# Queries and keys of three of four head groups as seven block products, in a transformer block of attention and feed-forward

## The chip, the cores and the metric

The kernel runs on one core of a Trainium2 chip. Five engines work side by side, each through its own list of instructions in order: TensorE (PE in the profile; PEld is its loading of weights), VectorE (DVE), ScalarE (ACT), GpSimd (POOL) and SyncE (SP), whose queue issues nearly all transfers. TensorE writes its results into PSUM, eight banks of 128 partitions x 512 floats; DVE and ACT read them there. The metric is the device time of one execution in microseconds, the median of several runs.

## The reference, cut to what matters

All numbers are 32-bit floats. B = 8 sequences of S = 1024 rows, D = 512 columns, H = 16 heads of 32.

```python
x = L0_attn_h                                     # (8, 1024, 512)
# attention, on the layer-normed x
qvk = (h @ Wqvk).reshape(b, s, 3, H, HD)
q, v, k = (qvk[:, :, 0], qvk[:, :, 1], qvk[:, :, 2])
scores = einsum('bshi,bthi->bsth', q, k) + causal_mask
weights = softmax(scores / sqrt(d), axis=2)
wv = einsum('bsth,bthi->bshi', weights, v).reshape(b, s, d)
x = x + layernorm(wv @ Wo)
# feed-forward, on the layer-normed x: W1, a sine transform with per-column parameters, relu, W2
x = x + layernorm(ffn(layernorm(x)))
```

The change is about `q` and `k`: for a group of four heads they are two products of the normed x (1024 x 512) with 128 columns of the weights each.

## The kernel before, in words

One sequence after the other; in each, attention over four groups of four heads (`attention`, L770), then the output projection and norm (`finish_block`, L871), then the feed-forward layer (`feed_forward`, L942). The normed x of a sequence lies transposed in SBUF, as `xnT[b, half]`: 128 partitions x 4 blocks of the contraction (`kc`) x 512 rows, for each half of the sequence. It is made during group 2 of the sequence before (`norm1`).

The order of the work is written by hand. Each engine does its instructions in the order in which the program issues them (`in_order`), and PE's stream is woven from generators: `advance(work, n)` issues the next n steps of one. `work` is the projection of the next group's queries, values and keys (`project_qkv`, L461); its steps are put between the steps of the present group's attention, so that PE has something to do while other engines read PSUM.

A group goes through these stages:

1. *The maxima* (`find_maxima`, L536). The softmax needs the maximum of each row beforehand. `run_unit` (L564) takes a *unit*: for the four heads of a group, 128 queries against up to 512 keys, four matmuls on 32 rows of the array each (L575), into two pairs of PSUM banks. A piece (i, c) is query block i against half c of the keys. DVE then reads the banks: a reduction where no mask is needed (L593), a masked one otherwise (L605). For the first half of the queries ACT also sums exponentials (L625). The units stand in four runs (`MAX_RUNS`, L520), and after run n come `MAX_FILL` steps of `work` (L529). The maxima are then split into three bfloat16 parts (`split`, L548; on POOL for the first half of the queries, on DVE for the second) and transposed on PE (`transpose_maxima`, L658, recorded at L115).
2. *The weights* (`weigh`, L667). A unit here is one or two key blocks against up to 512 queries: PE subtracts the transposed maxima (L681) and adds the scores (L692), ACT takes the exponential (L707), POOL zeroes what lies above the diagonal (L711). One unit later PE multiplies the weights with the values (`weighted_values`, L730), and DVE adds them up for the row sums (`add_weights`, L759). There are three units for the first half of the queries and seven for the second (`KEY_UNITS`).
3. Two units of the second half's maxima (`MAX_LATE`, L526: (7,1) and (7,0)) are done late, ahead of the first two units of weights. The first also has steps of `work` behind it. After the second one DVE splits the maxima (L556 to L562), and PE transposes the parts after the third unit of weights.
4. *The sums* (`whole`, L745): PE sums the weights over the partitions. This is issued after the first run of the next group's maxima, and ACT and DVE divide by it.

PSUM is given out by the program (`psum`, L85): it takes the free bank, or pair of banks, that was given back (`drained`, L104) longest ago in program order. A matmul into a bank waits until the last reader of what lay there has finished. In `project_qkv` the bank of a half of the queries or keys is taken, filled by four matmuls and emptied by ACT in one go (L477, L488).

The feed-forward layer already computes its two products by blocks, seven products for eight, with sums of the weights made once and stored (`w1_mixed`, `w2_mixed`), sums of the moving operand on POOL (`mix`, L925; `blocks`, L1121) and sums of the results on DVE (`add`, L1078 and L1155).

Weights come through a pool of 18 tiles (`wp`), fetched group by group (`fetch`, L142) and, for the feed-forward layer, as a stream up to 16 deep. Most large tiles come from the pool `pp` (19).

Of the kernel before, what the change touches and what calls it, by code (L numbers as in the profile page):

```python
# [32 lines left out]
def kernel(  # L33
# [34 lines left out]
    pp = ctx.enter_context(tc.tile_pool(name="pp", bufs=19))  # L68
# [3 lines left out]
    mixp = ctx.enter_context(tc.tile_pool(name="mixp", bufs=2))  # L72
# [61 lines left out]
    w2_mixed = dram.tile([NSTEP, len(PRODUCTS2), P, 2 * QUART], F32, tag="w2m", name="w2_mixed")  # L134
    wqvk_v = w_qvk.rearrange("(kc p) n -> p kc n", p=P)
# [6 lines left out]
    def fetch(b, g, queue=nc.sync):  # L142

        for part in (0, 1, 2):
            w_of[b, g, part] = w_tile([KC, P], "wqvk")
            c0 = part * D + g * P
            queue.dma_start(w_of[b, g, part], wqvk_v[:, :, c0 : c0 + P])

# [250 lines left out]

    moments_ahead = {}  # L400
# [60 lines left out]
    def project_qkv(b, g):  # L461
# [11 lines left out]
        def queries_or_keys(n, half):  # L473
            pq = psum([P, HALF])
            for kc in range(KC):
# [9 lines left out]
                if kc == 1:  # L485
                    yield True
# [3 lines left out]
            yield True  # L490

        def values(t0):
# [13 lines left out]
            drained(pv)  # L506
            yield True

        yield from queries_or_keys(0, 0)
        yield from values(0)  # L510
        yield from queries_or_keys(1, 0)
        yield from queries_or_keys(0, 1)
        yield from queries_or_keys(1, 1)
        for t0 in (2, 4, 6):
            yield from values(t0)

# [5 lines left out]
        (((6, 0),), ((4, 1), (6, 1))),  # L524
    )
    MAX_LATE = (((7, 1),), ((7, 0),))  # L526


    MAX_FILL = ((3, 2, 2, 2), (1, 2, 2, 2))  # L529
# [240 lines left out]
    def attention(b, wvT, after):  # L770
# [24 lines left out]
        for g in range(NG):  # L795
            more, first = after(g)
            mT, later = find_maxima(b, g, work, sums, more if first is None else iter(()))
            mTs = [mT]
            at = 0
            for c in range(2):  # L800
# [3 lines left out]
                for u, keys in enumerate(units):  # L804
                    later(at)
                    weights, placed = weigh(b, g, c, keys, mTs[c])
                    if at < 2:
                        advance(work)
                    if at == 2:
# [8 lines left out]
                    if c and u >= len(units) - 2:  # L818
# [52 lines left out]
    def finish_block(b, half, wvT, x2T, mixed, out_w):  # L871
# [3 lines left out]
        mixed[half] = mixp.tile([P, 3, 2, QUART], F32, tag="mix", name=f"mix_{b}_{half}")  # L875
# [49 lines left out]
        def mix(t):  # L925
# [6 lines left out]
            m1, m2, m4 = (mixed[half][:, n, :, t * P : (t + 1) * P] for n in range(3))  # L932
# [9 lines left out]
    def feed_forward(b, x2T, mixed, before, between):  # L942
# [49 lines left out]
        def product(bank, s, name, first=False):  # L992
# [7 lines left out]
                "4": m[:, 2],  # L1000
                "5": m[:, 0],
                "6": m[:, 1],
# [249 lines left out]
        finish(before)  # L1252
        units = second()
        advance(units)
        for s, quota in enumerate(SECOND):
# [3 lines left out]
            for n, more in enumerate(quota):  # L1259
# [9 lines left out]
                if s == STEPS and n == 3 and b + 1 < B:  # L1269
                    fetch(b + 1, 1)  # L1270
        finish(measuring)
        while len(quarters) > 1:
            advance_ends(1)
# [5 lines left out]
    for _ in range(TPB):  # L1279
        advance(work)  # L1280
# [75 lines left out]
```

## Time and profile before

| | |
|---|---|
| median of 3 runs | 3681.8 us (3679.7 to 3681.83) |
| the profiled execution | 3681.3 us, its span 3679.6 us |
| mean granted TensorE clock | 0.997 |
| matmuls of queries and keys (L477) | 481.3 us busy, 512 matmuls of 512 columns (recorded as 1024) |
| score matmuls for the maxima (L575) | 322.0 us |
| DVE's reading of them (L593, L605) | 309.8 and 432.5 us |
| one attention group of sequence 2 | 53.84 us, of which PE 53.61, DVE 39.93, ACT 32.55, POOL 10.14 busy |

A 32-bit matmul is recorded as two instructions, so the counts of PE are twice those of the program. Busy time of PE is the time in which any matmul is under way; the four matmuls of a unit, on 32 rows each, run side by side. A row of a timeline gives start, length, engine, line, operation, what it writes and reads, and how many instructions were merged; in brackets stand the idle time before it and the engine that ended it.

### The profile page before, as it was taken

Reading aid. Unit: us, or ns where it says so; the run is one execution under the profiler, and the core shown is the slowest. Engines: PE = TensorE matmul, PEld = TensorE weight load, DVE = VectorE, ACT = ScalarE, POOL = GpSimd, SP = SyncE. Lnnn points to the kernel's source line nnn. Section 1 sums busy time; section 2 is a strip of 40 time slices with the busy share of each in tenths; the row PEclk is TensorE's granted clock in tenths of the full one; section 3 lists DMA queues with packets and bytes.
Section 4 is the critical chain, followed back from the end, with each engine's and each line's share of the span. In section 5 each row is a group of like instructions: output and inputs, shape, how many; then the busy total and the mean of one; then the engine's idle time right before and its main releaser. Section 6 shows DMA issues by size and latency. Waiting matters only on the chain.

```text
span 3679.6 us, 61558 instructions
## 1 busy us (share of the span) xinstructions
PE 3601.1 (98%) x22721; PEld 2357.4 (64%) x22721; DVE 2680.4 (73%) x5571; ACT 1408.2 (38%) x2708; POOL 1133.8 (31%) x1740
## 2 busy tenths in 40 slices
PE   8999999999999999999999999999999999999998
PEld 4447864478654786548854488544885458854587
DVE  5877867678676786767867678776787767777775
ACT  4552135621355213652146521465114642156410
POOL 2333432134311343113431234222342223422243
PEclk9999999999999999999999999999999999999999
DMA  4444751047510574105841068310683116820176
GB/s 137 142 141 132 243 192 34 20 146 249 175 41 10 158 258 154 41 10 172 266 132 41 13 185 269 112 41 18 198 275 92 38 33 199 262 70 13 47 220 197
DMA packets 305084, 476.21 MB, mean 129 GB/s; under 512 B 29136, under 2 KB 90640, under 8 KB 304784
## 3 DMA queue, kind: packets, MB, share of 16 engines
q1 hardware_dynamic: 302624, 470.44, 40.8%
q8 instruction: 181, 2.97, 0.3%
q10 hardware_dynamic: 2160, 1.84, 0.2%
q14 instruction: 119, 0.97, 0.1%
HBM read 440.70 MB, written 31.46 MB: 128 GB/s over the span
## 4 chain that ended last, share of the span: by engine, by line
PE 83%; DVE 11%; ACT 2%; POOL 2%; issue 1%; DMA 0%; POOLq 0%; DVEq 0%; SPq 0%; ACTq 0%
PE banks L1144 16%; PE banks L1009 15%; PE banks L477 13%; PE banks L575 8%; PE banks L730 7%; PE banks L692 7%; PE banks L497 7%; PE banks L897 6%; PE banks L681 3%; PE banks L115 2%; DVE u L1036 2%; DVE hid L1052 2%; DVE u L1030 1%; PE banks L745 1%; DVE hid L1058 1%; ACT w L707 1%
## 5 line engine op out<-in xcount | busy, mean ns | idle before, releaser
L707 ACT ACTIVATE w<-banks 128x1024 f32<-128x1024 f32 (+1 forms) x640 | 566.6, 939 | 296.1 <-PE banks L692 296.0
L759 DVE TENSOR_TENSOR w<-w 128x1024 f32<-128x1024 f32 (+3 forms) x400 | 421.9, 1099 | 186.7 <-PE banks L730 151.8
L711 POOL TENSOR_SCALAR_AFFINE_SELECT w<-w 128x256 f32<-128x256 f32 x512 | 287.3, 578 | 847.2 <-ACT w L707 839.8
L605 DVE CUSTOM_DVE_ANT_0 es<-banks,mask 128x128 f32<-128x128 f32 (+3 forms) x1024 | 432.5, 485 | 102.6 <-PE banks L575 102.6
L1009 PE MATMUL banks<-x2T,wm 128*128 128x256 f32 x2048 | 477.3, 381 | 28.1 <-DVE u L1079 13.6
L477 PE MATMUL banks<-xnT,wqvk 128*128 128x512 f32 x1024 | 481.3, 609 | 0.7 <-ACT xnT L342 0.7
L1144 PE MATMUL banks<-wm,hm 128*128 128x256 f32 x2048 | 470.4, 380 | 2.3 <-POOL hm L1125 2.3
L1037 ACT ACTIVATE u<-u 128x1024 f32<-128x1024 f32 x128 | 135.3, 1057 | 852.1 <-DVE u L1036 803.5
L1009 PEld LDWEIGHTS banks<-x2T,wm 128*128 128x128 f32 x2048 | 386.7, 190 | 91.0 <-DVE u L1079 16.8
L1144 PEld LDWEIGHTS banks<-wm,hm 128*128 128x128 f32 x2048 | 388.0, 190 | 56.4 <-POOL hm L1125 5.5
L593 DVE TENSOR_REDUCE mx<-banks 128x1 f32<-128x512 f32 (+1 forms) x384 | 309.8, 862 | 109.1 <-PE banks L575 109.1
L1144 PE MATMUL banks<-wm,hid 128*128 128x256 f32 x1536 | 357.7, 379 | 0.0
L1009 PE MATMUL banks<-mix,wm 128*128 128x256 f32 x1536 | 354.6, 380 | 2.3 <-DVE u L1079 2.3
L1125 POOL TENSOR_TENSOR hm<-hid 128x256 f32<-128x256 f32 x256 | 204.0, 797 | 456.2 <-DVE hid L1058 437.9
L477 PEld LDWEIGHTS banks<-xnT,wqvk 128*128 128x128 f32 x1024 | 182.8, 190 | 239.1 <-issue 184.5
L692 PE MATMUL banks<-q,k 32*128 32x512 f32 (+3 forms) x3072 | 329.6, 491 | 0.0
L730 PE MATMUL banks<-w,v 128*32 128x512 f32 (+3 forms) x3072 | 318.5, 495 | 5.4 <-POOL w L711 5.4
L1009 PEld LDWEIGHTS banks<-mix,wm 128*128 128x128 f32 x1536 | 291.1, 190 | 50.6 <-issue 7.6
L575 PE MATMUL banks<-k,q 32*128 32x512 f32 (+3 forms) x3072 | 322.0, 513 | 0.4 <-DVE mx L605 0.2
L1144 PEld LDWEIGHTS banks<-wm,hid 128*128 128x128 f32 x1536 | 292.4, 190 | 39.1
L625 ACT ACTIVATE es<-es,mx 128x512 f32<-128x512 f32 (+3 forms) x512 | 279.6, 550 | 2.1 <-DVE mx L605 2.1
L497 PEld LDWEIGHTS banks<-wqvk,xnT 128*128 128x128 f32 x2048 | 239.3, 192 | 51.6 <-issue 24.4
(114 smaller groups left out, 4322.9 us busy)
## 6 DMA issues: line engine op xcount, KB each, us to landing
wm<-w_mixed SPq DMA_DIRECT2D x1344, 256.0 KB, 3.1
xin<-in_L_attn_h_dram SPq DMA_DIRECT2D x112, 256.0 KB, 3.8
wqvk<-in_L_attn_Wqvk_dram SPq DMA_DIRECT2D x93, 256.0 KB, 5.2
out_dram<-x SPq DMA_DIRECT2D x64, 256.0 KB, 2.1
x<-in_L_attn_h_dram SPq DMA_DIRECT2D x60, 256.0 KB, 3.1
w_mixed<-w_t SPq DMA_DIRECT2D x56, 256.0 KB, 3.0
wo<-in_L_attn_Wo_dram SPq DMA_DIRECT2D x32, 256.0 KB, 5.0
w_t<-in_L_ffn_W_dram SPq DMA_DIRECT2D x32, 128.0 KB, 4.0
```

Source lines behind the costliest of these rows:

```text
L477: nc.tensor.matmul(pq, w_of[b, g, 2 * n][:, kc, :], xnT[b, half][:, kc, :], start=(kc == 0), stop=(kc == KC - 1),)
L497: nc.tensor.matmul(pv[:, t - t0, :], xnT[b, t // TPB][:, kc, (t % TPB) * P : (t % TPB + 1) * P], w_of[b, g, 1][:, kc, :], start=(kc == 0), ...
L575: nc.tensor.matmul(scs[j // 2][:, j % 2, at : at + n], queries[r, i * P : (i + 1) * P], keys[r, k0 : k0 + n], start=True, stop=True,)
L593: nc.vector.tensor_reduce(out=mx[:, m], in_=sc[:, m, cols], op=ALU.min, axis=mybir.AxisListType.X,)
L605: nc.vector.tensor_tensor_reduce(out=es[:, m, cols], in0=sc[:, m, cols], in1=mask[:, HALF - n :], scale=1.0, scalar=FMAX, op0=ALU.add, op1 ...
L692: nc.tensor.matmul(sts[j // 2][:, j % 2, cols], all_keys[r, kb * P : (kb + 1) * P], all_queries[r, q0 : q0 + n], start=False, stop=True,)
L707: in_order(nc.scalar.activation(w[:, :, :width], st[:, :, :width], AF.Exp, scale=-1.0))
L711: select = nc.gpsimd.affine_select(out=square, in_=square, compare_op=ALU.is_ge, fill=0.0, base=0, pattern=[[0, 2], [1, P]], channel_multi ...
L730: nc.tensor.matmul(acc[r, HALF - n :], v[b, g][:, kb, r], weights[j // 2][:, j % 2, cols], start=first and k == 0, stop=last and k == len( ...
L759: in_order(nc.vector.tensor_add(t[:, :, q], t[:, :, q], w[:, :, cols]))
L1009: nc.tensor.matmul(bank[:, n, :], w[:, n, kc, :], moving[:, kc, :], start=first and kc == 0 and n == 0, stop=kc == 1 and n == 1, skip_grou ...
L1144: nc.tensor.matmul(region, a[:, n], w[:, n], start=start and n == 0, stop=last and n == 1, skip_group_check=True,)
```

## The change

For groups 1 to 3 of every sequence, queries and keys are computed together. With the two halves of the sequence, the two halves of the contraction, and queries and keys as the two halves of the result, they are a product of two 2 x 2 block matrices, and the change computes it as seven block products (two matmuls of 512 columns each) with sums of blocks before and after, instead of eight:

- the sums of the x blocks (`mix_x`): four tiles, made once for a sequence by eight POOL subtractions, at the end of the feed-forward layer of the sequence before; they stay for three groups;
- the sums of the weight blocks (`mix_weights_of_group`): made once, in the first sequence, by four POOL operations for each group, and stored in DRAM; later sequences load them as two more tiles with a group's weights;
- the sums of the results (`quarters`): PE accumulates in place in three banks, `one`, `two` and `three`, over four steps; `one` is held over two steps, `two` over four, `three` over three. DVE makes five additions from PSUM, ACT three copies for four before. Group 0 is computed as before.

The steps of `work` are regrouped: there is no step of half a projection any more, one step holds two block products (or one and two blocks of values), and `MAX_FILL` gives one step to each run (two to the first, in group 0). Values for rows 0 to 255 become the first step, which is issued with the last unit of weights of the group before; the step that stood with the second-last unit is gone, and so is the step between the first and second late unit.

One unit of the maxima, (6,0), leaves the fourth run and becomes a third late unit, issued behind the second unit of weights and the last values; the split of the second half's maxima follows it.

The feed-forward layer's sums of x move from a pool of their own to `pp`, which grows from 19 to 24 tiles.

```diff
@@ project_qkv
+        def quarters():
+            ...
+            one = psum([P, HALF])
+            product(one, wq, 0, xnT[b, 0][:, :2, :], True)
+            in_order(nc.scalar.copy(p1, one))
+            two = psum([P, HALF])
+            product(two, s12, 2, t2, True)
+            add(u2, two, p1)
+            in_order(nc.scalar.activation(u2s, u2, AF.Copy, scale=-QSCALE))
+            yield True
+            product(one, wq, 2, xnT[b, 0][:, 2:, :])
+            in_order(nc.scalar.activation(queries[:, near], one, AF.Copy, scale=-QSCALE))
+            drained(one)
+            three = psum([P, HALF])
+            product(three, s12, 0, t1, True)
+            yield True
+            product(two, s34, 0, t3)
+            add(u3, two, p1)
+            add(keys[:, far], three, u3)
+            values(2)
+            yield True
+            product(two, wk, 2, t4)
+            add(keys[:, near], two, p1)
+            drained(two)
+            product(three, s34, 2, xnT[b, 1][:, 2:, :])
+            in_order(
+                nc.vector.scalar_tensor_tensor(
+                    queries[:, far], three, -QSCALE, u2s, ALU.mult, ALU.add
+                )
+            )
+            drained(three)
+            yield True
+
+        values(0)
+        yield True
+        if g == 0:
+            ...
+        else:
+            yield from quarters()
+        for t0 in (4, 6):
+            values(t0)
+            yield True
@@
-        (((6, 0),), ((4, 1), (6, 1))),
+        (((4, 1), (6, 1)),),
     )
-    MAX_LATE = (((7, 1),), ((7, 0),))
-    MAX_FILL = ((3, 2, 2, 2), (1, 2, 2, 2))
+    MAX_LATE = (((7, 1),), ((7, 0),), ((6, 0),))
+    MAX_FILL = ((2, 1, 1, 1), (1, 1, 1, 1))
@@ attention
-                    later(at)
+                    if at < 2:
+                        later(at)
                     weights, placed = weigh(b, g, c, keys, mTs[c])
-                    if at < 2:
+                    if at == 1:
                         advance(work)
+                        later(at + 1)
...
-                    if c and u >= len(units) - 2:
+                    if c and u == len(units) - 1:
                         advance(work)
```

## The prediction

> **What bounds the kernel now.** I read the page first (engine shares, then the chain that ended last), then cut one attention group of sequence 2 (53.84 us, 1014.98 to 1068.82) into windows, then read the order in time of TensorE (PE) and VectorE (DVE) in it, and last the idle times of PE with the granted clock.
>
> ```profile
> PE 3601.1 (98%) x22721; PEld 2357.4 (64%) x22721; DVE 2680.4 (73%) x5571; ACT 1408.2 (38%) x2708; POOL 1133.8 (31%) x1740
> ...
> PE 83%; DVE 11%; ACT 2%; POOL 2%; issue 1%; DMA 0%; POOLq 0%; DVEq 0%; SPq 0%; ACTq 0%
> ```
>
> PE is busy 98% of the span: work taken from PE is worth its full duration only while no new wait takes its place. The windows of the group (columns: length, then busy time and count of PE, weight loads, DVE, ACT, POOL, then the granted PE clock):
>
> ```profile
> 1014.98:1020.97 5.99, 5.99 (x58) 3.28 (x57) 4.76 (x20) 3.05 (x10) 0.00 (x0) 1.00 0.00 0
> 1020.97:1026.54 5.57, 5.57 (x37) 2.73 (x33) 4.87 (x12) 4.27 (x14) 0.00 (x0) 1.00 0.00 0
> 1026.54:1032.11 5.57, 5.57 (x37) 2.51 (x33) 5.17 (x20) 3.46 (x12) 0.00 (x0) 1.00 0.13 34
> 1032.11:1037.80 5.69, 5.69 (x33) 3.57 (x29) 4.39 (x18) 2.01 (x7) 1.44 (x6) 1.00 0.21 60
> 1037.80:1049.10 11.30, 11.30 (x125) 6.91 (x124) 6.95 (x18) 6.06 (x9) 2.82 (x8) 1.00 0.15 42
> 1049.10:1068.80 19.70, 19.47 (x180) 6.71 (x176) 13.77 (x14) 13.70 (x16) 5.88 (x9) 1.00 0.13 45
> ```
>
> The first four windows are the maxima stage. PE never waits there, but DVE is busy 4.4 to 5.2 of some 5.6 us: the two run in step, and PE is covered only because it has projections to do (L477, L497) while DVE reads the scores. The order in time shows how tight this is:
>
> ```profile
> 1019.04 2.00 PE L575 MATMUL banks<-k,q 32*128 32x512 f32 x16
> 1020.97 3.70 PE L477 MATMUL banks<-xnT,wqvk 128*128 128x512 f32 x8
> 1024.60 2.00 PE L575 MATMUL banks<-k,q 32*128 32x512 f32 x24
> ...
> 1041.93 1.14 PE L575 MATMUL banks<-k,q 32*128 32x512 f32 x8
> ...
> 1047.77 0.40 PE L115 MATMUL banks<-ident_h,parts_q 128*128 128x128 bf16 x4
> ```
>
> ```profile
> 1020.20 2.42 DVE L593 TENSOR_REDUCE mx<-banks 128x1 f32<-128x512 f32 x3 [0.60 <-PE banks L575]
> ...
> 1043.08 2.42 DVE L593 TENSOR_REDUCE mx<-banks 128x1 f32<-128x512 f32 x3 [1.59 <-PE banks L575]
> ...
> 1045.54 0.23 DVE L556 TENSOR_TENSOR mx<-mx 128x16 f32<-128x16 f32 x1
> ...
> 1047.08 0.20 DVE L560 CAST parts_q<-mx 128x16 bf16<-128x16 f32 x1
> ```
>
> A unit of four heads takes PE 0.96 us (1041.93 to 1042.89); DVE begins 1.16 us after the unit's start and reduces it in 2.42 us (0.6, 0.6, 1.2 for the pair); the split into three parts ends at 1047.28. So the last late unit has its parts ready 5.35 us after it starts, and PE's transposition of them (L115) comes 5.84 us after: 0.5 us to spare.
>
> Last, two rows of what a wait costs besides itself. At 97.98 PE had stood idle 1.96 us (for a selection on POOL); 1.6 us later the granted clock is half for 3.4 us:
>
> ```profile
> 96.00:98.00 2.00, 0.04 (x4) 0.02 (x2) 1.60 (x3) 0.00 (x0) 2.00 (x3) 1.00 0.44 153
> 98.00:99.50 1.50, 1.50 (x20) 0.81 (x24) 1.50 (x2) 0.00 (x0) 1.50 (x2) 1.00 0.77 235
> 99.50:103.00 3.50, 3.50 (x19) 0.97 (x12) 3.50 (x16) 0.47 (x1) 0.45 (x1) 0.51 0.73 203
> ```
>
> The gaps of 1.69 and 1.70 us at the start of the feed-forward stage (eight of them, one for each sequence) are followed by no such fall.
>
> **What is removed.** A projection of 512 columns takes PE 3.63 us for four (1020.97 to 1024.60), 0.907 us each. Sixteen become fourteen in 24 groups (three in each of eight sequences): 48 x 0.907 = 43.6 us off PE. ACT loses one copy of four (0.60 us) for each, off the path.
>
> **What is added and moved, by the new program's order.** I count from the start of a middle group (t = 0), with the durations above.
>
> (1) Second unit pair of the maxima. The projections now keep two of the eight banks across the runs of score units (the block sums are built in place), before they kept none. In the new order unit (5,0) takes banks 2, 3 and 6, 7, and (3,0) takes 0, 1 and then 2, 3 again; before, (3,0) had four others. PE: run 0 1.08, sums 1.0, two products 3.63, so (5,0) starts at 5.7 and (3,0) could run from 6.7 to 7.65. DVE reads bank 2 until 7.5 and bank 3 until 8.1; the last head starts at 8.2 and ends at 9.05. Wait 1.4 us; the next projection, which needs the whole array, queues behind it.
>
> (2) Third run. (4,0) and (1,0)+(5,1) now use the same banks 0 to 3; before, disjoint ones. (4,0) starts 12.7, DVE reads it from 13.85 to 16.27; the second unit, which PE would do from 13.65 to 14.6, ends at 17.3. Wait 2.7 us.
>
> (3) The first transposition of the maxima: ACT's exponentials of that run now stand behind the copy of values (done 21.7), then 2.0 us of exponentials, 0.2 of Ln, 1.8 on POOL: 25.9 against PE's 25.75. Wait 0.2 us.
>
> (4) Late units (7,1) and (7,0) use the same four banks, and the values (2.0 us) that stood between them are moved behind the second. DVE needs 1.16 + 4 x 0.61 for the first; PE comes after 0.96 + 1.18: it waits 1.45 us, in all 32 groups (about 1.2 where the next sequence's transposes lie between).
>
> (5) The third late unit (6,0) with its split is now followed by one set of weighted values (1.0) and one weighing (0.65) only, and then the transposition. Ready 5.35 us after its start plus 0.1; PE is there after 0.96 + 1.0 + 0.65 = 2.6. Wait 2.85 us in the 24 groups g = 0, 1, 3; 1.85 at g = 2, where 1.04 us of transposes lies between. Queued behind: all of the second half's weighing.
>
> (6) At a group's end 3.63 us of projections became 1.98 of values. DVE's sums of weights end 7.0 us after the weighing of (5,7); PE asks for them after 1.0 + 0.65 + 1.98 + 1.43 + 1.08 = 6.15: 0.95 us, at the next two groups (g = 1, 2); between g = 2 and 3 the transposes cover it.
>
> The five new DVE operations of a group (0.69 us each, row L1079) fall into DVE's gaps: counted at nothing; without that cover 3.4 us a group. The unit taken out of the fourth run gives its 0.96 us back later, so it is neutral but for (5).
>
> By group: g = 0 1.4 + 2.7 + 0.2 + 1.45 + 2.85 = 8.6; g = 1 9.55; g = 2 1.4 + 2.7 + 0.2 + 1.2 + 1.85 + 0.95 = 8.3; g = 3 4.3. A sequence 30.75, eight of them 246 us.
>
> (7) Differences of x: eight POOL subtractions of 128x512, 1.27 us each (row L1225), at a sequence's end, where POOL has 20.4 of 37 us busy (1380 to 1417). Hidden by that idle time; bound from above, if each held up a block of the hidden layer: 10 us a sequence, 81 in all. I take 0. At the start they run beside 15 us of first projections: 0 to 5 us, I take 0. Two more weight loads of 256 KB for each group stand on SP behind all feed-forward weights, some 15 us ahead of use: 0. The block sums of the weights are made once (three times four POOL operations of 0.8 us, their stores on SP): behind them stands POOL's selection for the first values, some 6 us ahead of use: 0, at most 7. The tiles moved to the large pool leave 17 to 21 of its 24 to the work that had 19; the 17 fall in its last two steps, when most hidden tiles are used up: 0.
>
> (8) The clock. The waits of 2.7 and 2.85 us (six a sequence, 48) lie beyond the 1.96 us that halved it; a halving costs 1.7 us (half of 3.4). The clock record changes only on a raster of 3.41 us (half from 99.56 for one step and from 3400.25, 967 steps later, for three), so a wait must put about 1.96 us into one raster step: (3.41 - 1.96) + (2.8 - 1.96) = 2.3 of 3.41 positions, 67%; in (2) single heads work in between, so I take 60%: 48 x 0.6 x 1.7 = 49 us. Ends: 0, and 82 if all do.
>
> Against this row stands a rule. The Trainium skill, "TensorE: Matmul & The Clock Gate", Part 1 ("What's actually happening"), says that the clock falls to half after at least one idle window of about 3.4 us. By it none of my waits would cost more than itself and the sum would be 3884; by the row at 97.98 it is 3933.
>
> Sum against the profiled execution's own 3681.3 us (0.5 below the median of 3681.8): 3681.3 - 43.6 + 246 + 49 = **3933 us**, 6.8% slower.
>
> **Rivals.** A is the sum above: 47%.
> B, the waits come but the clock stays: 3681.3 - 43.6 + 246 = 3884. For it: the eight gaps of 1.7 us without a fall. 27%.
> C, the bank waits (1, 2, 4) are taken up, as a bank is set free by each reduction and PE has single heads to go on with; what stays is (5), 8 x (3 x 2.85 + 1.85) = 83: 3681.3 - 43.6 + 83 = 3721. Against it: PE keeps its order, and the whole-array projections stand behind. 10%.
> D, the other side: DVE has 14 us idle in a group and hides all reads, (5) too: 3681.3 - 43.6 = 3638. It decides where new waits fall below 1.82 us a group. Against it: the 5.35 us from unit to parts cannot shrink while the unit stands 2.6 us ahead. 4%.
> E, the clock falls after the 1.4 us waits as well, half of 14 a sequence: 112 x 0.5 x 1.7 = 95, or the subtractions of (7) are not hidden: 3980 to 4060. 12%.
>
> **Range and chances.** B and A with their sizes uncertain by a fifth of 246 (49 us) reach from 3835 to 3982; going towards E and somewhat towards C gives 3810 to 4020, which leaves out about 2 in 10. A measurement of this kernel can tell about 0.2% (7 us). Faster 0.04 (D), same 0.01, slower 0.95.
>
> **What would show it.** PE idle time rises from 79 us to over 250 and its busy time falls to some 3560; waits of the score matmuls and of the parts' transposition on DVE come up in PE's list of waits, some 24 x 4 and 32 x 2.8 us; the granted clock's mean falls below 0.99 (A) or stays at 0.997 (B). Wrong would be: the group after still at 52 us without idle PE (D), or the third run without a wait (C).

## The result: 3944.2 us, 7.1% slower

The changed kernel takes 3944.2 us (median of 4 runs, 3940.5 to 3947.5) against 3681.8 us before: 1.0713 times as long, 95% interval 1.0695 to 1.0732. The forecast was 3933. The profiled execution of the changed kernel has a span of 3938.8 us and a mean granted clock of 0.986 (before 3679.6 and 0.997).

From the page of the kernel after, engine shares, the chain that ended last, and two of its groups (busy time and mean ns of one, then the idle time before them):

```profile
PE 3742.9 (95%) x22625; PEld 2397.1 (61%) x22625; DVE 2772.5 (70%) x5691; ACT 1394.8 (35%) x2684; POOL 1224.7 (31%) x1816
...
PE 78%; DVE 14%; POOL 3%; ACT 3%; issue 2%; DMA 0%; SPq 0%; POOLq 0%; DVEq 0%; ACTq 0%
...
L672 PE MATMUL banks<-k,q 32*128 32x512 f32 (+3 forms) x3072 | 453.6, 533 | 29.2 <-DVE mx L690 29.1
...
L690 DVE TENSOR_REDUCE mx<-banks 128x1 f32<-128x512 f32 (+1 forms) x384 | 311.7, 862 | 172.9 <-PE banks L672 172.5
```

PE has 96 instructions fewer, and its busy time *rose* by 142 us, although some 44 us of products are gone. Most of the increase, 131.6 us, is in the score matmuls of the maxima (L672, L575 before, 322.0 us), whose number is the same; the scores and weighted values of the weights stage add 26 and 24.5 us. A unit is four heads on 32 rows of the array each; when two heads run and the other two wait for their banks, PE counts as busy. Only 29 us of these waits appear as idle time. So a share of 95% does not mean that PE is short of time, and the list of waits shows only part:

```profile
PE banks L114 <- DVE parts_q L657: 52.1, 25, 3.0
PE banks L672 <- DVE mx L690: 29.1, 49, 0.8
PE banks L1114 <- DVE u L1184: 19.2, 23, 1.7
```

Here are the windows of group 1 of sequence 2 in the kernel after, with the columns of the prediction's table (length, then busy time and count of PE, weight loads, DVE, ACT, POOL, and the granted clock):

```profile
1097.11:1102.82 5.71, 5.71 (x35) 2.13 (x33) 3.98 (x18) 1.81 (x3) 0.00 (x0) 1.00 0.01 3
1102.82:1110.00 7.18, 7.18 (x25) 2.72 (x25) 5.55 (x12) 6.17 (x21) 0.00 (x0) 1.00 0.08 20
1110.00:1118.39 8.39, 7.19 (x45) 4.21 (x44) 6.38 (x21) 1.80 (x6) 0.00 (x0) 1.00 0.17 47
1118.39:1123.26 4.87, 4.87 (x29) 2.21 (x29) 3.63 (x18) 2.56 (x10) 1.44 (x6) 1.00 0.12 36
1123.26:1138.29 15.03, 12.92 (x115) 7.89 (x112) 9.40 (x21) 6.29 (x9) 3.20 (x8) 1.00 0.33 108
1138.29:1160.13 21.84, 21.84 (x205) 8.37 (x205) 13.74 (x15) 13.47 (x16) 6.01 (x8) 0.92 0.01 5
```

Before, the maxima (the first four windows) took 22.82 us, the late units 11.30 and the weights 19.70. Now they take 26.15, 15.03 and 21.84: 9.2 us more, although PE has 1.82 us less to do. The three stages do not hold quite the same work in the two tables. If the late stage is taken from the first late unit to the values behind the transposition (1125.19 to 1139.83, the stretch that is 1037.80 to 1049.10 before), the stages take 28.08, 14.64 and 20.30 us. The weights also hold a half-rate step of the clock. In the maxima the second and the third window grew most. In order of time, PE in the second and third run and around the late units:

```profile
1102.82 3.62 PE L672 MATMUL banks<-k,q 32*128 32x512 f32 x16
1106.37 1.98 PE L544 MATMUL banks<-xnT,wqvk 128*128 128x512 f32 x4
...
1110.00 1.14 PE L672 MATMUL banks<-k,q 32*128 32x512 f32 x8
1111.90 1.29 PE L672 MATMUL banks<-k,q 32*128 32x256 f32 x4 [0.77 <-DVE mx L690]
1113.63 1.13 PE L672 MATMUL banks<-k,q 32*128 32x256 f32 x12 [0.44 <-DVE mx L690]
1114.69 1.98 PE L544 MATMUL banks<-xm,wmix 128*128 128x512 f32 x4
...
1125.19 1.14 PE L672 MATMUL banks<-k,q 32*128 32x512 f32 x8
...
1131.13 2.05 PE L530 MATMUL banks<-wqvk,xnT 128*128 128x128 f32 x16
1133.11 1.14 PE L672 MATMUL banks<-k,q 32*128 32x512 f32 x8
...
1138.29 0.40 PE L114 MATMUL banks<-ident_h,parts_q 128*128 128x128 bf16 x4 [1.97 <-DVE parts_q L657]
```

Two units that took 1.93 us (1019.04 to 1020.97 before) take 3.55 in the second run (1102.82 to 1106.37) and 4.69 in the third (1110.00 to 1114.69). From the last late unit (1133.11) to the transposition of its parts 5.18 us pass, though PE has 2.6 us of work. VectorE's side of that wait, in the same group:

```profile
1134.27 2.42 DVE L690 TENSOR_REDUCE mx<-banks 128x1 f32<-128x512 f32 x3 [2.95 <-PE banks L672]
1136.72 0.18 DVE L653 TENSOR_TENSOR mx<-mx 128x16 f32<-128x16 f32 x1
...
1138.03 0.20 DVE L657 CAST parts_q<-mx 128x16 bf16<-128x16 f32 x1
```

VectorE had stood idle for 2.95 us before the unit came, and then needs the 5 us that it always needed from the unit to its parts. PE follows 0.06 us after the last part.

### The profile page after: what moved, and what is told of

The parts are those of the page before. It is cut to its first block, busy times and chain, and to the rows that moved or that the text cites. A ratio compares the mean times of both kernels' runs of the same rounds, so it can differ in the third digit from the quotient of the medians.

```text
span 3938.8 us, 61451 instructions
## 1 busy us (share of the span) xinstructions
PE 3742.9 (95%) x22625; PEld 2397.1 (61%) x22625; DVE 2772.5 (70%) x5691; ACT 1394.8 (35%) x2684; POOL 1224.7 (31%) x1816
## 3 DMA queue, kind: packets, MB, share of 16 engines
q8 instruction: 180, 2.95, 0.3%
q10 hardware_dynamic: 2160, 1.84, 0.1%
## 4 chain that ended last, share of the span: by engine, by line
PE 78%; DVE 14%; POOL 3%; ACT 3%; issue 2%; DMA 0%; SPq 0%; POOLq 0%; DVEq 0%; ACTq 0%
PE banks L1249 15%; PE banks L1114 14%; PE banks L672 9%; PE banks L544 8%; PE banks L789 6%; PE banks L827 6%; PE banks L530 6%; PE banks L1002 5%; DVE mx L690 3%; PE banks L513 3%; PE banks L778 3%; DVE hid L1157 2%; PE banks L114 2%; DVE u L1141 2%; ACT w L804 2%
## 5 line engine op out<-in xcount | busy, mean ns | idle before, releaser
L672 PE MATMUL banks<-k,q 32*128 32x512 f32 (+3 forms) x3072 | 453.6, 533 | 29.2 <-DVE mx L690 29.1
L789 PE MATMUL banks<-q,k 32*128 32x512 f32 (+3 forms) x3072 | 355.6, 508 | 0.0
L827 PE MATMUL banks<-w,v 128*32 128x512 f32 (+3 forms) x3072 | 343.0, 506 | 12.3 <-POOL w L808 12.3
L672 PEld LDWEIGHTS banks<-k,q 32*128 32x128 f32 x3072 | 186.5, 189 | 223.8 <-DVE mx L690 93.5
L1249 PEld LDWEIGHTS banks<-wm,hid 128*128 128x128 f32 x1536 | 290.6, 190 | 43.6 <-issue 3.6
L530 PE MATMUL banks<-wqvk,xnT 128*128 128x128 f32 x2048 | 259.5, 280 | 0.0
L1114 PE MATMUL banks<-mix,wm 128*128 128x256 f32 x1024 | 241.9, 379 | 0.0
L1002 PE MATMUL banks<-wo,wvT 128*128 128x512 f32 x512 | 235.7, 600 | 3.2 <-DVE wvT L864 3.2
```

The costliest lines, as they stand in the source:

```text
L530: nc.tensor.matmul(pv[:, t - t0, :], xnT[b, t // TPB][:, kc, (t % TPB) * P : (t % TPB + 1) * P], w_of[b, g, 1][:, kc, :], start=(kc == 0), ...
L672: nc.tensor.matmul(scs[j // 2][:, j % 2, at : at + n], queries[r, i * P : (i + 1) * P], keys[r, k0 : k0 + n], start=True, stop=True,)
L789: nc.tensor.matmul(sts[j // 2][:, j % 2, cols], all_keys[r, kb * P : (kb + 1) * P], all_queries[r, q0 : q0 + n], start=False, stop=True,)
L827: nc.tensor.matmul(acc[r, HALF - n :], v[b, g][:, kb, r], weights[j // 2][:, j % 2, cols], start=first and k == 0, stop=last and k == len( ...
L1002: nc.tensor.matmul(y, wvT[:, kc, t * P : (t + 1) * P], out_w[kc], start=(kc == 0), stop=(kc == KC - 1),)
L1114: nc.tensor.matmul(bank[:, n, :], w[:, n, kc, :], moving[:, kc, :], start=first and kc == 0 and n == 0, stop=kc == 1 and n == 1, skip_grou ...
```

## The experiments

All ratios are against the kernel before, measured on the same chip (3681.4 to 3682.3 us). A steady sequence took 453.83 us before and takes 484.69 in the kernel after; its four groups 57.6, 53.8, 57.4 and 285.0 us, and 63.8, 63.0, 64.3 and 293.7 (the fourth with the feed-forward stage). "Half-rate steps" are steps of 3.41 us in the record of the granted clock, counted in the profiled execution: 4 before, 30 after. The profiled execution of the kernel after is the fastest of its four and has the highest mean clock (0.986; the others 0.982 to 0.984), so counts of steps are set against profiled times.

### The late unit, put back and taken alone

```diff
 e1_unit_back (from the kernel after)
-        (((4, 1), (6, 1)),),
+        (((6, 0),), ((4, 1), (6, 1))),
-    MAX_LATE = (((7, 1),), ((7, 0),), ((6, 0),))
+    MAX_LATE = (((7, 1),), ((7, 0),))
 e2_unit_alone (from the kernel before)
-        (((6, 0),), ((4, 1), (6, 1))),
+        (((4, 1), (6, 1)),),
-    MAX_LATE = (((7, 1),), ((7, 0),))
+    MAX_LATE = (((7, 1),), ((7, 0),), ((6, 0),))
 ... the third late unit is called behind the second unit of weights and the step of `work` after it
```

> The changed kernel, with unit (6,0) put back into the fourth run of the maxima; everything else as changed. Theory (the waits of the prediction): the wait for the second split, 2.6 us in three groups of a sequence and 1.3 in the one with transposes, goes, but the fourth run has two units on the same banks again and waits 2.8 us in the three groups with block products, as the third run does: 8 x (3 x 2.8 - 3 x 2.6 - 1.3) = -6 us, 3938, between 3915 and 3960 with the clock's halvings. Rival (the late unit is what costs, the banks do not): the whole of 8 x 9.1 = 73 us is saved, 3871.

Measured: 3953.7 us, 1.0739 (1.0721 to 1.0757), 46 half-rate steps. The wait for the late parts is gone from the list. In its place:

```profile
PE banks L672 <- DVE mx L690: 62.6, 96, 0.8
```

The listed wait of the maxima for their banks doubles (29.1 before this edit). Groups 0 to 2 of the sequence looked at (sequence 2) take 65.5, 64.9 and 65.4 us; the fourth gains 2.7. The 10 us that this edit costs lie in the clock, by this estimate: at 1.27 to 1.65 us for a step (measured below, in `e5_keep_busy`) the 16 steps more are 20 to 26 us, and the profiled executions differ by 14. Without them the kernel would be some 6 to 12 us shorter than the kernel after, near the 6 us of the theory. So in waits it makes little difference where the unit stands, since the place that it left is short of banks.

> The kernel before, with one part of the change alone: unit (6,0) becomes the third late unit, behind the second unit of weights and the values; projections, steps and banks stay as before. Theory: PE waits for the second split 2.6 us in three groups of a sequence and 1.3 in the one with transposes, 8 x 9.1 = 73 us, and some of these waits halve the clock (1.3 us each, up to 24): 3755 to 3787. Rival (a late unit is covered, and the waits come from the block products alone): within 10 us of 3682.

Measured: 3790.9 us, 1.0296 (1.0280 to 1.0311), groups 60.5, 58.3, 59.5 and 287.9 us (sequence 4). The late unit alone, with all eight projections left as they were, costs 109 us, of which 16 half-rate steps more are some 20 to 26. PE's list says where:

```profile
PE banks L115 <- DVE parts_q L560: 51.6, 25, 3.0
```

That is 25 waits of some 2 us, as in the kernel after (52.1). In the kernel before the same line reads

```profile
PE banks L115 <- DVE parts_q L560: 1.5, 3, 0.5
```

The result lies 4 us above the theory's range, and the rival's no change is 109 us off. What the late unit costs depends on its company: 109 us alone, next to nothing in waits where the banks are short.

### One bank less held across the third run

```diff
 e3_one_pair (from the kernel after, in quarters)
+            product(two, s34, 0, t3)
+            add(u3, two, p1)
+            yield True
             three = psum([P, HALF])
             product(three, s12, 0, t1, True)
-            yield True
-            product(two, s34, 0, t3)
-            add(u3, two, p1)
             add(keys[:, far], three, u3)
             values(2)
```

> The changed kernel, with two of the seven block products exchanged in order (the one that u3 needs comes into the second step, the one in the third bank into the third), so that the third bank is the neighbour of the second and three pairs stay free in every run instead of two; the work is the same. Theory (banks): the wait in the third run falls from 2.8 to that of the second run, 1.6 us, in 24 groups: -27 us and a few us of halved clock, 3905 to 3920. Rival (DVE's rate, not the banks, sets the pace of the maxima): within 8 us of 3944.

Measured: 3898.2 us, 1.0588 (1.0572 to 1.0604). In group 1 of sequence 2 the third run is over 16.45 us after the group's start, 17.58 in the kernel after, and the group takes 62.1 us, 0.9 less. The banks do set the wait. The gain in the medians, 46 us, is larger than I had worked out (24 to 39). The profiled executions differ by 40 us. The half-rate steps (26 for 30) explain 5 to 7 of that. Where no step falls in, a group is some 1.1 us shorter (62.6 us for 63.7 in group 0), 27 us over 24 groups, as expected.

### The subtractions of x

```diff
 e4_no_mix_x (from the kernel after)
-        mixing_x = mix_x(b + 1) if b + 1 < B else iter(())
+        x_mixed[b + 1] = x_mixed[b]
+        mixing_x = iter(())
```

> The changed kernel without the POOL subtractions that make the differences of x for sequences 1 to 7; those of sequence 0 are used for all, so queries and keys are wrong from sequence 1 on, and the same matmuls are done. Theory (the subtractions delay the blocks of the hidden layer on POOL and slow DVE): the extra 2 to 3 us at the end of each feed-forward layer go, 7 x 2 to 3 = 14 to 21 us: 3923 to 3930. Rival (they are hidden, as the prediction had it): within 8 us of 3944.

Measured: 3929.8 us, 1.0675 (1.0659 to 1.0691). The interval with the feed-forward stage falls from 293.7 to 291.1 us where no half-rate step falls in, so GpSimd's subtractions at the end of a sequence cost 2.6 us each time, some 18 in all (seven times). The median gains 14, and the profiled execution only 4, as it has 41 half-rate steps. In the kernel after, PE waits at that place for 1.86 and 0.91 us where it waited 0.56 and 0.29 before:

```profile
1475.69 1.99 PE L1114 MATMUL banks<-x2T,wm 128*128 128x256 f32 x8 [1.86 <-DVE hid L1184]
...
1490.21 3.72 PE L1249 MATMUL banks<-wm,hm 128*128 128x256 f32 x16 [0.91 <-POOL hm L1230]
```

The second wait is for GpSimd's next sum of hidden blocks, which stands behind a subtraction. The first is for VectorE, whose operations take longer beside a subtraction. One subtraction of the kernel after, VectorE beside it, and the same two rows of VectorE in `e4_no_mix_x`, where GpSimd is idle:

```profile
1469.74 1.71 POOL L432 TENSOR_TENSOR xm<-xnT,xm 128x512 f32<-128x512 f32 x1
...
1469.22 1.10 DVE L1339 TENSOR_TENSOR x<-x,yb 128x512 f32<-128x512 f32 x1
1470.85 1.81 DVE L1157 SCALAR_TENSOR_TENSOR hid<-u,coef,hid 128x512 f32<-128x512 f32 x2
...
2429.62 0.69 DVE L1339 TENSOR_TENSOR x<-x,yb 128x512 f32<-128x512 f32 x1
2430.83 1.40 DVE L1157 SCALAR_TENSOR_TENSOR hid<-u,coef,hid 128x512 f32<-128x512 f32 x2
```

### PE kept busy in its waits

```diff
 e5_keep_busy (from the kernel after)
+    def keep_busy(times):
+        spare = psum([P, HALF])
+        for _ in range(times):
+            in_order(nc.tensor.matmul(spare, ident_h, mask, start=True, stop=True))
+        drained(spare)
 ... between the units of the third run, g < 3
+                keep_busy(3)
 ... ahead of the second transposition of the maxima
+                        keep_busy(8)
```

> The changed kernel with products added that nobody reads, in the two longest waits of a group: eight bf16 products of 128x512 into a spare bank (some 0.22 us each, 1.76 us in all) ahead of the second transposition of the maxima, where PE stands 2.58 us for the late unit, and three (0.66 us) between the units of the third run, where it stands 2.76 us. The results are the reference's. Theory (a wait ends when VectorE ends, whatever PE does meanwhile, and the waits also cost half-rate steps of the clock): the waits end at the same moments, the added 8 x (4 x 1.76 + 3 x 0.66) = 72 us of work costs nothing, and what the 26 added half-rate steps cost, 1.27 us each, goes: 3911, and 3944 if all of them stay; range 3905 to 3950. Rival (PE's own work is the bound there, and what I read as waits is time that PE needs): the added work counts in full, 3944 + 72 = 4016. Between them, if the products cost what they overhang at g = 2, where the wait is 1.34 us: 8 x 0.4 = 3 us more.

Measured: 3917.3 us, 1.0646 (1.0628 to 1.0664). More work on PE, and 27 us less. The same group in this kernel starts at 1080.02:

```profile
1097.61 1.98 PE L544 MATMUL banks<-xm,wmix 128*128 128x512 f32 x4
...
1116.03 1.14 PE L672 MATMUL banks<-k,q 32*128 32x512 f32 x8
...
1119.18 1.90 PE L761 MATMUL banks<-mask,ident_h 128*128 128x512 bf16 x7
1121.21 0.40 PE L114 MATMUL banks<-ident_h,parts_q 128*128 128x128 bf16 x4
```

The third run ends 17.59 us after the group's start (17.58 in the kernel after), the transposition comes 41.19 us after it (41.18). In this group the 1.9 us of added products vanish in the wait, to a hundredth of a microsecond: PE's own work is not the bound there. In group 2, where the wait is shorter, they do not. PE at that transposition, in the kernel after (group start 1160.13) and with PE kept busy (1141.77):

```profile
1203.32 0.40 PE L114 MATMUL banks<-ident_h,parts_q 128*128 128x128 bf16 x4 [0.64 <-ACT w L804]
...
1182.61 1.90 PE L761 MATMUL banks<-mask,ident_h 128*128 128x512 bf16 x7
1184.35 0.39 PE L114 MATMUL banks<-ident_h,parts_q 128*128 128x128 bf16 x4
```

It comes 43.19 us after the group's start in the kernel after, which has a half-rate step in the third run, and 42.58 here, which has none. Ahead of the added products, at the first transposition, the difference is 1.65 us (27.56 against 25.91): that is the step. Behind them 0.61 is left, so they took 1.04 back, in seven groups 7 us.

What did change for the better is the clock: 9 half-rate steps for 30. The 27 us are net of those 7, so 21 steps were worth some 34 us, 1.6 each, near half of their length (1.71). What a step costs depends on where it falls: 1.65 us in the third run of group 2, 1.27 in the weights of group 1 (63.02 us against 61.75), and 0.13 at the end of the feed-forward stage in this run (293.80 against 293.67).

### A finer order, to mend the waits

With the causes named, I looked for an order that keeps the seven products and loses less. `e6_fine` has seven rounds, one unit and one product each, instead of four runs of up to two units and two products; `e7_values_first` moves one step in it.

```diff
 e6_fine (from the kernel after)
-        (((5, 0),), ((3, 0),)),
-        (((4, 0),), ((1, 0), (5, 1))),
-        (((4, 1), (6, 1)),),
+        (((5, 0),),), (((3, 0),),), (((4, 0),),), (((1, 0), (5, 1)),), (((6, 0),),), (((4, 1), (6, 1)),),
-    MAX_FILL = ((2, 1, 1, 1), (1, 1, 1, 1))
+    MAX_FILL = ((3, 1, 1, 1, 1, 1, 1), (1,) * 7, (1,) * 7, (1, 0, 2, 0, 2, 0, 2))
 quarters: one product for each step, all of the first five in one pair of banks
+            pair = psum([P, 2, HALF])
+            one, two = pair[:, 0], pair[:, 1]
 feed_forward: the subtractions in the last step only
-                if s >= STEPS - 1:
-                    advance(mixing_x)
+                if s == STEPS and 1 <= n <= 4:
+                    advance(mixing_x, 2)
 e7_values_first (from e6_fine)
+            if g == 1:
+                values(0)
+                yield True
             product(two, s34, 0, t3)
```

> The seven products kept, their order against the maxima mended: one product after each maxima unit (not two after each pair of units), all sums in one pair of banks, so that the second half of a unit uses the banks that the unit before used first; unit (6,0) back among the maxima of the first half, the values back between the two late units, three projections at a group's end, and the subtractions of x only in the last step of the feed-forward stage. Theory (the loss is the bank waits, the late unit, POOL's selections at the group's end and the half-rate steps): by hand some 0.7 us of waits are left in a group of three (0.2 to 1.2), against 1.82 us of PE work saved in it: 3681.8 - 43.6 + 24 x 0.7 + 0 to 20 for the subtractions = 3655 to 3675, range 3640 to 3720. Rival (seven products cost more than they save whatever the order, since VectorE has five more operations of 0.69 us a group in the stage where it is nearly full): 24 x 5 x 0.69 = 83 us on the path, 3681.8 - 43.6 + 83 = 3721, and above it up to 3800.

Measured: 3723.1 us, 1.0113 (1.0098 to 1.0129). Of the 262 us that the change lost, 221 are back, but it is still slower than before, and the rival's 3721 fits. The groups of sequence 3 speak against the rival's mechanism: 63.7, 54.3, 57.8 and 284.9 us, so most of the loss is in the first group alone (60.7 to 63.7 us in the steady sequences, 57.6 before), where PE has this (the list of the order in time):

```profile
1427.08 1.88 PE L547 MATMUL banks<-xm,wmix 128*128 128x512 f32 x4
1432.01 3.75 PE L547 MATMUL banks<-xm,wmix 128*128 128x512 f32 x4 [3.05 <-issue]
```

```profile
1431.16 0.17 DVE L310 BATCH_NORM_AGGREGATE mv<-st 128x2 f32<-128x6 f32 x1
1431.26 0.66 DVE L565 TENSOR_TENSOR u<-banks,p 128x512 f32<-128x512 f32 x1
```

The next product goes into the bank that VectorE's sum has to read first, and that sum stands behind the norm of the last rows and the masked maxima. (The profile names no engine for this wait; the next run settles it.) The fourth interval is back at 284.9, as before the change: the subtractions cost nothing that shows where they now stand.

> The finer order with one change: in the first group of a sequence the first values stand between the second and the third product, where PE stood idle 3.05 us (VectorE's sum that frees the bank came behind the norm of the last rows and the masked maxima). Theory (that wait, and the half-rate step after it, make the finer order's first group 6.1 us longer than before's): the values take 2.05 us of PE's wait, 1.0 is left, which is too short for a half-rate step (1.3): 7 sequences x (2.05 + 1.3) = 23 us, 3723 - 23 = 3700, range 3690 to 3707. Rival (the values are then missing where they stood, between the late units, and VectorE is as late there): 3715 to 3725.

Measured: 3696.5 us, 1.0039 (1.0024 to 1.0054), the first group 58.5 us instead of 60.7 to 63.7; no gap over 0.54 us is left there, and the half-rate steps are 3.

### Why the finer order still loses: rounds or VectorE

```diff
 e8_adds_late (from e7_values_first): the values among the maxima, the last two products behind them
+            for t0 in (2, 4, 6):
+                values(t0)
+                yield True
             three = psum([P, HALF])
             product(three, s12, 0, t1, True)
 e9_before_fine (from the kernel before): MAX_RUNS and MAX_FILL in seven rounds, as in e6_fine, nothing else
+    MAX_FILL = ((3, 1, 1, 1, 1, 1, 1), (1,) * 7)
```

> As the run with the values first, and the last two products (with two of the five sums on VectorE) change places with values, so that they stand at the late units, and values among the maxima. In the finer order VectorE is busy 21.9 of the 23.6 us of the maxima (93%), before 19.4 of 24.2 (80%). Theory one (VectorE's sums are what keeps the finer order from its 1.82 us a group; its units of scores take 9.9 us of PE's time in a group against 8.8 before): 1.38 us less on VectorE there, some 1 us less a group, 24 us less than the run before: 3665 to 3685. Theory two (the many changes between 32-row units and products over the whole array cost it, whatever VectorE does): as the run before, 3690 to 3707; and up to 3720 if the product's bank, now held over a late unit, makes the late units wait.

Measured: 3724.4 us, 1.0115 (1.0100 to 1.0130). A middle group takes 55.6 us for 54.3, and 1.4 us of it is PE's time in the weights beside the late units (the subtraction of the maxima, 4.06 for 2.68): the time lies 4 us above the highest that either theory gave, for a bank held over a late unit. That bank took any gain, so this run says nothing on VectorE's sums.

> The kernel before with the finer order alone: eight whole projections, no sums of quarters, each maxima unit followed by half a projection. It adds no work to any engine. Theory two above (the changes between units and products cost PE: in the finer order a group's score units take 1.09 us more, its seven products 0.09 us more each, the weighing 0.6 more): 32 groups x 1.2 to 2.3 = 38 to 74 us, 3720 to 3756. Theory one (VectorE's sums cost it): nothing, 3682, up to 3690.

Measured: 3721.2 us, 1.0107 (1.0090 to 1.0123). This kernel has eight projections, no sums and the same work on every engine as before, and loses 39 us: 1.2 us for each of 32 groups. Its rounds in order of time:

```profile
1489.03 1.14 PE L578 MATMUL banks<-k,q 32*128 32x512 f32 x8
1490.10 1.98 PE L477 MATMUL banks<-xnT,wqvk 128*128 128x512 f32 x4
1492.02 1.14 PE L578 MATMUL banks<-k,q 32*128 32x512 f32 x8
```

A round of one unit and two matmuls takes 2.99 us; twice that is 5.98. The coarse order did two units and four matmuls in 5.56 (1019.04 to 1024.60 in the prediction's rows). So each extra round costs some 0.4 us, three of them 1.2. The Trainium skill, "TensorEngine Tiling (Array Packing)", "Key Properties", states that a change of the tiling mode drains TensorE, and gives no price. The trace fits that, and no run here shows the drain itself; a round has two such changes, some 0.2 us for each here.

The seven products save 1.82 us a group, and the order that frees them of waits takes 1.2 of that back.

### Fewer rounds, and sums off VectorE

```diff
 e10_coarser (from e7_values_first): five rounds, and three sums moved
+        (((4, 0),), ((1, 0), (5, 1))),
+        (((6, 0),), ((4, 1), (6, 1))),
-            add(u3, two, p1)
+            in_order(nc.scalar.copy(u3, two))
+            add_on_pool(u3, u3, p1)
             ... the same for u2s and the first half of the keys
 e11_sums_on_pool (from e7_values_first): seven rounds, these three sums and the second half of the keys moved
-            add(keys[:, far], three, u3)
+            in_order(nc.scalar.copy(keys[:, far], three))
+            add_on_pool(keys[:, far], keys[:, far], u3)
```

> The seven products with the order of the run with the values first, but only five rounds of maxima instead of seven (once the pair of banks of the sums is free, two units and then two products and values again), and three of the five sums moved from VectorE: ScalarE takes the product out of its bank and GpSimd adds, which also frees the bank without VectorE. Theory (what the run with the values first lacks to 3681.8 - 43.6 is 0.39 us for each round more, as the fine order of the kernel before shows, and VectorE late at the late units): 24 x 2 x 0.39 = 19 us less than 3696.5, 8 x 0.5 for the wait in the first group, and up to 24 x 0.8 for VectorE's 2.1 us a group: 3655 to 3678, faster than before. Rival (GpSimd's additions of 1.27 us come in the way of VectorE or of its own selections, or the coarser rounds bring back a bank wait of 1.4 us or more): 3690 to 3730.

Measured: 3732.4 us, 1.0137 (1.0120 to 1.0154). That is 2 us above the rival's range, and its second half, a bank wait from the coarser rounds, is there at 1.28 us. The one sum left on VectorE between two products of the same bank stands behind two units now:

```profile
1508.00 1.98 PE L547 MATMUL banks<-xnT,wmix 128*128 128x512 f32 x4 [1.28 <-DVE k L565]
```

> The run with the values first (seven rounds, 3696.5), and four of the five sums moved from VectorE: ScalarE copies the product out, GpSimd adds in SBUF (1.27 us, it has some 20 us idle in this stage). Nothing else is moved. Theory (after the rounds, 1.2 us a group, what is left of that kernel's distance to 3681.8 - 43.6 = 3638 is VectorE, late by its 3.45 us of sums, at the late units): a middle group then takes 53.84 - 1.82 + 1.2 = 53.2 instead of 54.34, the other two lose 0.8 and 0.3 to 1: 8 x 1.7 to 3 = 14 to 24 us less: 3672 to 3683, about the kernel before. Rival (VectorE is not what the late units wait for): 3690 to 3705.

Measured: 3686.5 us, 1.0014 (1.0005 to 1.0023). Ten of the 14 to 24 us came, so the time lies between the two forecasts, 3.5 us from each. The kernel ends 5 us above the kernel before: little, but the interval lies above 1, and each sequence is 0.6 us longer (454.4 against 453.8). A middle group takes 54.1 us against 53.8: the seven products take 13.4 us of PE's time in order (14.6 for the eight), the score units 9.7 for 8.8, the weights 12.6 for 12.0. The first two numbers are mostly the rounds: in `e9_before_fine` the score units take 9.45 us, and the projections 15.2 for 14.6. The last 0.6 us is in every kernel with the seven products in the finer order but not in `e9_before_fine`, and what causes it stays open. No version here beats the kernel before.

## Why the prediction was right, and where it was wrong

Its direction and size hold: 3944 against 3933, inside the range. Step by step, for steady sequences (predicted, then measured):

| step | predicted | measured |
|---|---|---|
| (1) second run | 1.4 us | 1.62 |
| (2) third run | 2.7 | 2.76 |
| (3) first transposition | 0.2 | 0 |
| (4) after (7,1); at g = 2 | 1.45; 1.2 | 1.59; 1.1 |
| (5) parts of (6,0); at g = 2 | 2.85; 1.85 | 2.58; 1.34 |
| groups 0, 1, 2, added waits | 8.6, 9.55, 8.3 | 9.6, 9.7, 7.0 |
| group 3 without the feed-forward stage | 4.3 | 4.1 |
| sequence, all waits of groups | 30.75 | 30.4 |
| (7) subtractions of x, all sequences | 0 | about 18 |
| (8) clock | 49 | 33 to 43 |

The single steps are from group 1 of sequence 2 (and group 2 of it); the groups' added waits are their growth in sequence 4, plus the projections and values that they do less than before, less the half-rate step, where one falls in (1.27 in group 1, 1.65 in group 2). Groups 1 and 2 do 1.82 us less. Steps of `work` also moved across the borders of groups: group 0 does 3.46 us less, and group 3 does 1.65 more.

- **Steps 1, 2, 4 and 5** were read from the order of the banks and VectorE's durations, and each lies within some 0.5 us. Steps 2 and 5 are shown by more than their sizes: one bank less shortens the third run (e3), the late unit alone brings its wait into the kernel before (e2), and work put into the waits of group 1 costs nothing (e5). Steps 1 and 4 had no run of their own; they rest on the rows and went together with the others when the order was mended (e6).
- **Step 6** had the right size and the wrong mechanism. VectorE's sums of the weights were not late. The 1 us at a group's end comes because 1.65 us less work stands ahead of the weighted values, so that they now wait for GpSimd's selection (here at the end of group 0 of sequence 3):

```profile
1574.95 1.41 PE L827 MATMUL banks<-w,v 128*32 128x512 f32 x8 [0.26 <-POOL w L808]
...
1580.69 1.17 PE L827 MATMUL banks<-w,v 128*32 128x256 f32 x8 [0.56 <-POOL w L808]
```

  So it falls at the end of groups 0 and 1, where the prediction had it at the start of groups 1 and 2: group 0 is 1.0 us above its forecast, group 2 is 1.3 below.
- **Step 7** failed. I had called eight subtractions hidden because GpSimd was busy for only 20.4 of 37 us. A share of idle time says nothing of the moment: a subtraction of 1.27 us in front of a sum that PE needs next delays it, and VectorE's operations beside a subtraction took longer (1.10 us for 0.69). They cost 2.6 us a sequence (e4), within the bounds given (0 to 10), and nothing once they stand in the last step (e6).
- **Step 8** was somewhat over-sized: 26 half-rate steps more, 29 predicted, at 1.27 to 1.65 us each (e5), where I had put half of 3.41. That the number is near is partly luck: I had put three to four in each sequence, and there are 7, 7, then 2 in each of five sequences, and 6 in the last. The page's rule that I weighed against the row (the Trainium skill, "TensorE: Matmul & The Clock Gate", Part 1, "What's actually happening": half rate after at least one idle window of about 3.4 us) does not agree with this case. Around the wait of 1.97 us the kernel after has

```profile
1136.00:1139.34 3.34, 1.37 (x24) 0.56 (x20) 2.45 (x8) 1.08 (x2) 0.85 (x2) 1.00 0.70 250
1139.34:1142.75 3.41, 3.41 (x32) 0.97 (x24) 0.00 (x0) 0.56 (x1) 0.00 (x0) 0.50 0.02 5
```

  PE was busy for 41% of the stretch ahead, and the clock fell for the next 3.41 us all the same. By the page's rule the sum was 3884 (rival B), 60 us short, of which the clock is some 33 to 43.
- **What would show it**: I had expected PE's busy time to fall to 3560 us and its idle time to rise above 250. Busy time rose to 3743 and idle time only to 196. The mean clock, 0.986, was as case A had it. The mistake is one of reading: waits inside a unit of four heads count as busy.

With the measured terms: 3681.3 - 43.6 + 243 + 18 + (33 to 43) = 3932 to 3942, where the profiled execution took 3940.5 us. The subtractions, left out, and the clock, put too high, are errors of opposite sign; that they nearly cancel is luck.

## What to carry to other kernels

Before work is taken off the busiest engine, look for a partner that runs in step with it. Here each round was PE writing banks and VectorE emptying them, so 1.8 us off PE bought nothing while banks held longer and a unit issued later brought in 9 us of waits a group. Before an accumulation is kept in PSUM over several steps, write out which banks the neighbouring steps take and when each is read to the end; before a piece of work is called hidden, look at what is queued behind it at that moment, not at the engine's share. A finer interleaving can remove such waits, but here each extra change between units of 32 rows and whole-array products cost 0.4 us a round, and that has to be set against the saving first.

## What the runs showed of the hardware

- A half-rate step of the clock follows a wait of 1.97 us (the rows above), while gaps of 1.70 us at the start of each feed-forward stage are followed by none in either kernel. The length of one idle gap does not settle it. In the kernel after, a stretch of 3.41 us with 1.20 us of listed idle time, in the third run of a group 2, is followed by a step. One with 1.84 us, at the end of the feed-forward stage, is not:

```profile
1173.48:1176.89 3.41, 2.21 (x16) 0.83 (x12) 2.42 (x3) 1.34 (x4) 0.00 (x0) 1.00 0.29 81
1176.89:1180.30 3.41, 3.41 (x14) 1.63 (x11) 2.56 (x15) 0.00 (x0) 0.00 (x0) 0.50 0.02 5
...
1473.85:1477.26 3.41, 1.57 (x7) 1.41 (x8) 3.34 (x6) 0.00 (x0) 3.33 (x5) 1.00 0.97 321
1477.26:1480.67 3.41, 3.41 (x17) 3.00 (x17) 3.34 (x5) 0.00 (x0) 1.14 (x1) 1.00 0.73 258
```

  In the first stretch two of four heads run while the other two wait for banks, and PE counts as busy. Whether the clock goes by such half-filled work was not tested.
- One half-rate step cost 1.27 and 1.65 us in two places of a group, and 0.13 at the end of the feed-forward stage.
- In the profiled execution of the kernel after, the steady sequences take 484.69 us, 142.0 times the 3.4133 us of the clock's raster, and the half-rate steps begin at the same places of each sequence (1139.34 and 1176.89, then 1624.03 and 1661.58). Other kernels with steps do not fall into such a rhythm: in `e3_one_pair` the steady sequences take 478.47 to 482.89 us.
- Filling waits with work of no use made the kernel 27 us faster.
